# Transposing activations with VectorE and SBUF to SBUF transfers in place of TensorE transposes

## The chip, the cores and the metric

The kernel runs on one core of a Trainium2 chip. The metric is device time in microseconds (us): medians over several executions. Where two kernels are compared, the ratio is the mean time of one kernel's fast runs over that of the other's fast runs of the same rounds, with a 95% interval; it is therefore not quite the ratio of the medians that are quoted beside it.

## The reference, cut to what matters

Four layers of a graph network act on `x` of shape (32, 512, 128), all fp32: 32 graphs ("batches") of 512 nodes ("tokens") with 128 features.

```python
h = maximum(layernorm(x), 0)                      # ahead of every layer
# layer 0: attention weights A from adj, the same for every batch
x += (A * I) @ h @ W[0] + (A * (1 - I)) @ h @ W[1] + bias
# layer 1: Chebyshev hops of adj
x += relu(concat(h, adj^T h, (2 adj^2 - 1)^T h, ...) @ Theta1 + bias)
# layer 2: messages
f  = relu(h @ psi + psi_b);  m = (adj * adj)^T f
x += relu(concat(m, h) @ phi1 + phi1_b) @ phi2 + phi2_b
# layer 3: attention with a mask
s  = tanh((h @ q) @ (h @ k)^T / sqrt(128) / 8) * 8
e  = exp(s) * adj;  x += (e / e.sum(-1)) @ h @ v
```

Every product with a weight matrix sums over the features. By the code, the kernel's matmul call sums over the partitions of its operands, so `h`, which the layer norm leaves with tokens on the partitions, must first be transposed so that features are on the partitions.

## The kernel before

Sixteen pairs of batches pass through each layer, one step of a generator at a time, so that the engines work on several pairs at once. `P` and `D` are 128, `N` is 512, `NT = N // P` is 4. A pair in a layer needs 8 transposes of 128x128: TensorE makes four into one PSUM bank, and ScalarE copies the bank out to the tile `hT`, in which the 512 tokens of a batch are contiguous.

```python
def transposed(src, name, copy):
    p = bank(f"p_{name}")                          # one PSUM bank, 128 x 512 fp32
    for t in range(NT):
        nc.tensor.transpose(p[:, blk(t)], src[:, t, :], ident)
    s = work.tile([P, N], F32, tag="hT", name=name, bufs=8)
    copy(s, p)
    return s

def projected(name, *terms):                       # stationary: a block of hT
    p = bank(name)
    for t in range(NT):
        for i, (hT, w) in enumerate(terms):
            nc.tensor.matmul(p[:, blk(t)], hT[:, blk(t)], w, start=(i == 0),
                             stop=(i == len(terms) - 1))
    return tiles(p)
# ... (cut)
def layer0_first(q):                               # four pairs ahead of layer0(q)
    ln_stats(q)
    yield
    h = normed(q)
    yield
    hT = [transposed(h[:, b], f"hT0_{q}_{b}", nc.scalar.copy) for b in range(2)]
    yield
    # ... pg = projected(f"p_g_{q}_{b}", (hT[b], w0[:, 1, :])), copied to g by VectorE
def layer0(q):
    # ... hd[b] = hT[b] * adiag on GpSimd; x + bias on GpSimd
    # ... po += attT-block @ g  (p_l, 128x256), po += hd-block @ w0[:, 0, :]  (p_l, 128x128)
def layer2(q):
    h = normed(q)
    yield
    hT = [transposed(h[:, b], f"hT2_{q}_{b}", nc.scalar.copy) for b in range(2)]
    yield
    # ... pf = projected(f"p_feat_{q}_{b}", (hT[b], psi)); msgT = mixed(feat, sq)
    #     ph  = phi1[:, 1, :] @ hT[b]    moving: 512 columns of hT   (p_phi)
    #     ph += phi1[:, 0, :] @ msgT[b]
def layer3(q):
    # ... pp = qk @ hT[b]                moving: 512 columns of hT   (p_qkh)
    #     pv = projected(f"p_hv_{q}_{b}", (hT[b], vw))
    #     ps = hT[b]-block @ qkh         stationary: hT              (p_score)
```

In the profile a matmul has a stationary operand of 128x128, read by a weight load (LDWEIGHTS), and a moving operand, whose columns the MATMUL instruction reads. `hT` is used as both. Such a product of fp32 operands in the source is two instructions in the profile (`p_feat`: 128 products, x256), a transpose is one (`p_hT`: 512, x512).

Of the kernel before, what the change touches and what calls it, by code (L numbers as in the profile page):

```python
# [9 lines left out]
F32 = mybir.dt.float32  # L10
# [3 lines left out]
AX = mybir.AxisListType  # L14

P = 128
NEG = 9000000000000000.0
EPS = 1e-5
EARLY = 4
# [3 lines left out]
def kernel(  # L23
# [27 lines left out]
    nc = tc.nc  # L51
    B, N, D = x.shape
    NT = N // P
# [4 lines left out]
    const = ctx.enter_context(tc.tile_pool(name="const", bufs=1))  # L58
    xpool = ctx.enter_context(tc.tile_pool(name="xpool", bufs=NQ))
    stats = ctx.enter_context(tc.tile_pool(name="stats", bufs=NQ + 2))  # L60
    psum = ctx.enter_context(tc.tile_pool(name="psum", bufs=8, space=bass.MemoryType.PSUM))
    work = ctx.enter_context(tc.tile_pool(name="work", bufs=4))

    def bank(name):
        return psum.tile([P, 512], F32, tag="bank", name=name)

    def tiles(ap):
        return ap.rearrange("p (t f) -> p t f", f=D)

    def blk(t):  # L70
        return slice(t * P, (t + 1) * P)


    adj_s = const.tile([P, NT, N], F32, name="adj_s")
    adj_r = adj.rearrange("(t p) j -> p t j", p=P)
    for t in range(NT):
        nc.sync.dma_start(adj_s[:, t, :], adj_r[:, t, :])
# [24 lines left out]
    w0 = const.tile([P, 2, D], F32, name="w0")  # L102
# [12 lines left out]
    th = load_rows(theta, "th")  # L115
    b1 = load_bcast(bias_l1, "b1")
    psi = load_rows(psi_w, "psi")[:, 0, :]
    psib = load_bcast(psi_b, "psib")
    phi1 = load_rows(phi1_w, "phi1")
    phi1b = const.tile([P, 1], F32, name="phi1b")  # L120
    nc.sync.dma_start(phi1b, phi1_b.rearrange("(p o) -> p o", o=1))
    phi2 = load_rows(phi2_w, "phi2")[:, 0, :]
    phi2b = load_bcast(phi2_b, "phi2b")
    vw = load_rows(v_w, "vw")[:, 0, :]
# [3 lines left out]
    prep = prep_scope.enter_context(tc.tile_pool(name="prep", bufs=1))  # L128
# [10 lines left out]
    ident = const.tile([P, P], F32, name="ident")  # L139
# [42 lines left out]
                nc.scalar.activation(h[:, b], h[:, b], AF.Relu)  # L182
        return h

    def transposed(src, name, copy):
        p = bank(f"p_{name}")
        for t in range(NT):
            nc.tensor.transpose(p[:, blk(t)], src[:, t, :], ident)  # L188
        s = work.tile([P, N], F32, tag="hT", name=name, bufs=8)
        copy(s, p)  # L190
        return s

    def mixed(h, mat, tag, name, copy):

# [4 lines left out]
        copy(s, p)  # L199
        return s  # L200

    def projected(name, *terms):

        p = bank(name)
        for t in range(NT):
            for i, (hT, w) in enumerate(terms):
                nc.tensor.matmul(p[:, blk(t)], hT[:, blk(t)], w, start=(i == 0),  # L207
                                 stop=(i == len(terms) - 1))
        return tiles(p)

# [3 lines left out]
    def layer0_first(q):  # L214
        ln_stats(q)
        yield
        h = normed(q)
        yield
        hT = [transposed(h[:, b], f"hT0_{q}_{b}", nc.scalar.copy) for b in range(2)]
        yield  # L220
        g = work.tile([P, NT, 2, D], F32, tag="g", name=f"g_{q}", bufs=4)
        for b in range(2):
            pg = projected(f"p_g_{q}_{b}", (hT[b], w0[:, 1, :]))
            nc.vector.tensor_copy(g[:, :, b, :], pg)
        early[q] = hT, g

# [6 lines left out]


    adjT = const.tile([P, NT, N], F32, name="adjT")
    cheb = const.tile([P, NT, N], F32, name="cheb")

    def fillers():

# [41 lines left out]
    for t in range(NT):  # L281
        for s in range(t + 1):
            nc.tensor.matmul(pi[:, t : t + 1], upto[:, s, blk(t)], rch[:, s : s + 1],
                             start=(s == 0), stop=(s == t))
    pc = bank("p_count")
    for t in range(NT):
        nc.tensor.matmul(pc, rch[:, t : t + 1].to_broadcast([P, P]), upto[:, t, :],
                         start=(t == 0), stop=(t == NT - 1))
# [7 lines left out]
    for t in range(NT):  # L296
        s = prep.tile([P, NE], F16, tag="lt", name=f"lt_{t}", bufs=2)
# [5 lines left out]
    pg = []  # L303
    for kk in range(NK):
# [3 lines left out]
        for t in range(NT):  # L308
            nc.tensor.matmul(pb[:, kk : kk + 1], of_row[:, t, blk(kk)], befh[:, t : t + 1],
                             start=(t == 0), stop=(t == NT - 1))  # L310
# [10 lines left out]
    for kk in range(NK):  # L321
        s = prep.tile([P, N], F16, tag="scr", name=f"scr_r{kk}", bufs=2)
# [4 lines left out]
    for kk in range(NK):  # L327
        w = prep.tile([P, N], F32, tag="scan", name=f"scan_{kk}", bufs=2)
# [6 lines left out]
                                ecol[:, kk : kk + 1], OP.is_equal, OP.mult)  # L335


    att = prep.tile([P, NT, N], F32, name="att")
    diag = prep.tile([P, NT, P], F32, name="diag")
    neg_max = prep.tile([P, NT], F32, name="neg_max")  # L340
    total = prep.tile([P, NT], F32, name="total")
# [21 lines left out]
        nc.vector.tensor_sub(att[:, t, blk(t)], att[:, t, blk(t)], diag[:, t, :])  # L363

    fill(2 * EARLY + 2)
    attT = const.tile([P, NT, N], F32, tag="att_sq", name="attT")
    transpose_square(att, attT, "attT")

    adiag = const.tile([P, N], F32, name="adiag")
    p = bank("p_adiag")  # L370
    for t in range(NT):
        nc.tensor.matmul(p[:, blk(t)], ones, diag[:, t, :], start=True, stop=True)
    nc.scalar.copy(adiag, p)
    for _ in filler:
        pass

# [18 lines left out]

    def layer0(q):
        hT, g = early.pop(q)
        hd = []
        for b in range(2):
            hd.append(late.tile([P, N], F32, tag="mT", name=f"hd_{q}_{b}"))  # L400
            nc.gpsimd.tensor_mul(hd[b], hT[b], adiag)
        nc.gpsimd.tensor_add(xt[q], xt[q], b0[:, None, None, :].to_broadcast([P, 2, NT, D]))
        yield
        for t0 in range(0, NT, 2):
            po = bank(f"p_l0_{q}_{t0}").rearrange("p (t b f) -> p t b f", t=2, b=2)
            for i in range(2):
                for s in range(NT):
                    nc.tensor.matmul(po[:, i], attT[:, s, blk(t0 + i)], g[:, s], start=(s == 0), stop=False)  # L408
                for b in range(2):
                    nc.tensor.matmul(po[:, i, b], hd[b][:, blk(t0 + i)], w0[:, 0, :], start=False,  # L410
                                     stop=(b == 1))
            xv = xt[q][:, :, t0 : t0 + 2, :].rearrange("p b t f -> p t b f")
            nc.vector.tensor_add(xv, po, xv)
        ln_stats(q)

    def layer1(q):
        h = normed(q)
        yield
        hT = [transposed(h[:, b], f"hT1_{q}_{b}", nc.scalar.copy) for b in range(2)]
        x1T, x2T = [], []  # L420
        for b in range(2):
            x1T.append(mixed(h[:, b], adj_s, "mT", f"x1T_{q}_{b}", nc.vector.tensor_copy))
            x2T.append(mixed(h[:, b], cheb, "x2T", f"x2T_{q}_{b}", nc.scalar.copy))
        yield
        for b in range(2):
            po = projected(f"p_l1_{q}_{b}", (hT[b], th[:, 0, :]), (x1T[b], th12[:, 0, :]),
                           (x2T[b], th12[:, 1, :]))
            y = late.tile([P, NT, D], F32, tag="y", name=f"y1_{q}_{b}", bufs=3)
            nc.vector.tensor_add(y, po, spread(b1, NT))
            nc.vector.scalar_tensor_tensor(xt[q][:, b], y, 0.0, xt[q][:, b], OP.max, OP.add)  # L430
        ln_stats(q)

    def layer2(q):
        h = normed(q)
        yield
        hT = [transposed(h[:, b], f"hT2_{q}_{b}", nc.scalar.copy) for b in range(2)]
        yield
        feat = []
        for b in range(2):
            pf = projected(f"p_feat_{q}_{b}", (hT[b], psi))  # L440
            feat.append(late.tile([P, NT, D], F32, tag="y", name=f"feat_{q}_{b}", bufs=3))
            nc.vector.tensor_add(feat[b], pf, spread(psib, NT))
            nc.scalar.activation(feat[b], feat[b], AF.Relu)
        yield
        msgT = [mixed(feat[b], sq[0], "mT", f"msgT_{q}_{b}", nc.vector.tensor_copy) for b in range(2)]
        nc.gpsimd.tensor_add(xt[q], xt[q], phi2b[:, None, None, :].to_broadcast([P, 2, NT, D]))  # L446
        yield
        h1T = []
        for b in range(2):
            ph = bank(f"p_phi1_{q}_{b}")  # L450
            nc.tensor.matmul(ph, phi1[:, 1, :], hT[b], start=True, stop=False)  # L451
            nc.tensor.matmul(ph, phi1[:, 0, :], msgT[b], start=False, stop=True)  # L452
            h1T.append(late.tile([P, N], F32, tag="x2T", name=f"h1T_{q}_{b}"))
            nc.scalar.activation(h1T[b], ph, AF.Relu, bias=phi1b)
        yield
        for b in range(2):
            po = projected(f"p_l2_{q}_{b}", (h1T[b], phi2))
            nc.vector.tensor_add(xt[q][:, b], po, xt[q][:, b])
        ln_stats(q)

    def layer3(q):
        h = normed(q, on_act=False)
        yield
        hT = [transposed(h[:, b], f"hT3_{q}_{b}", nc.scalar.copy) for b in range(2)]
        yield
        for b in range(2):
            pp = bank(f"p_qkh_{q}_{b}")
            nc.tensor.matmul(pp, qk, hT[b], start=True, stop=True)  # L468
            qkh = late.tile([P, N], F32, tag="mT", name=f"qkh_{q}_{b}")
            nc.vector.tensor_copy(qkh, pp)  # L470

            pv = projected(f"p_hv_{q}_{b}", (hT[b], vw))
            hv = late.tile([P, NT, D + 1], F32, tag="hv", name=f"hv_{q}_{b}", bufs=3)
            nc.gpsimd.memset(hv[:, :, D : D + 1], 1.0)
            nc.vector.tensor_copy(hv[:, :, :D], pv)
            yield
            ex = late.tile([P, NT, N], F32, tag="ex", name=f"ex_{q}_{b}", bufs=3)
            for t in range(NT):
                ps = bank(f"p_score_{q}_{b}_{t}")
                nc.tensor.matmul(ps, hT[b][:, blk(t)], qkh, start=True, stop=True)  # L480
                nc.scalar.activation(ex[:, t, :], ps, AF.Tanh, scale=1.0 / (8.0 * math.sqrt(D)))  # L481
            for t in range(NT):
                nc.scalar.activation(ex[:, t, :], ex[:, t, :], AF.Exp, scale=8.0)  # L483
# [17 lines left out]
    sq = []  # L501

    def square():
        sq.append(const.tile([P, NT, N], F32, tag="att_sq", name="sq"))
        nc.gpsimd.tensor_mul(sq[0], adj_s, adj_s)
        yield

# [44 lines left out]
```

## Time and profile before

| | before |
|---|---|
| time, median of the first 3 runs | 1100.01 us (1099.19 to 1100.29) |
| TensorE busy | 1072.8 of 1096.7 us |
| VectorE, ScalarE, GpSimd busy | 489.5, 471.7, 213.3 us |

Three more of before are needed for comparison with what comes later. The first is from the chain of waits in order of time (start us, us, what), the second from the groups by form (busy us, mean ns, then idle time ahead and its cause), the third from the waits of TensorE (us in total, times, longest):

```profile
646.43 0.86 PE p_phi L451 x2
```

```profile
L207 PEld LDWEIGHTS p_feat<-psi,hT 128*128 128x128 f32 x256 | 31.0, 192 | 7.7 <-issue 7.2 <-ACT hT L190 0.5
```

```profile
PE p_g L207 <- ACT hT L190: 3.0, 3, 1.8
```

Two 512-column matmuls that stream `hT` take 0.86 us. A weight load from `hT` lasts 192 ns. In the whole run TensorE waits for transposed tiles for only 3.0 us ahead of `p_g` and 0.2 us ahead of `p_feat`.

### The profile page before, as it was taken

Reading aid. Unit: us, or ns where it says so; the run is one execution under the profiler, and the core shown is the slowest. Engines: PE = TensorE matmul, PEld = TensorE weight load, DVE = VectorE, ACT = ScalarE, POOL = GpSimd, SP = SyncE. Lnnn points to the kernel's source line nnn. Section 1 sums busy time; section 2 is a strip of 40 time slices with the busy share of each in tenths; the row PEclk is TensorE's granted clock in tenths of the full one; section 3 lists DMA queues with packets and bytes.
Section 4 is the critical chain, followed back from the end, with each engine's and each line's share of the span. In section 5 each row is a group of like instructions: output and inputs, shape, how many; then the busy total and the mean of one; then the engine's idle time right before and its main releaser. Section 6 shows DMA issues by size and latency. Waiting matters only on the chain.

```text
span 1096.7 us, 13885 instructions
## 1 busy us (share of the span) xinstructions
PE 1072.8 (98%) x5446; PEld 747.8 (68%) x5446; DVE 489.5 (45%) x1160; ACT 471.7 (43%) x997; POOL 213.3 (19%) x179
## 2 busy tenths in 40 slices
PE   5899999999999999999999999999999999999997
PEld 3579999985656656556566655666667777777776
DVE  8715555332322322323233333445475655554443
ACT  5734433502322323223264444443286656565553
POOL 3334444220000000000021111100023222222232
PEclk9999999999999999999999999999999999999999
DMA  9400000000000000000000000000000000000001
GB/s 274 115 1 1 1 1 1 1 1 1 1 1 1 1 1 1 1 1 1 1 1 1 1 0 1 1 1 1 1 11 30 30 30 30 30 30 29 30 30 39
DMA packets 37489, 19.90 MB, mean 18 GB/s; under 512 B 1840, under 2 KB 36912, under 8 KB 37424
## 3 DMA queue, kind: packets, MB, share of 16 engines
q1 hardware_dynamic: 37424, 19.01, 6.3%
q8 instruction: 43, 0.70, 0.3%
q14 instruction: 22, 0.18, 0.1%
HBM read 10.62 MB, written 8.39 MB: 17 GB/s over the span
## 4 chain that ended last, share of the span: by engine, by line
PE 94%; SPq 2%; issue 1%; ACT 1%; DMA 1%; POOL 0%; DVE 0%; POOLq 0%; DVEq 0%
PE p_l L207 10%; PE p_msgT L197 10%; PE p_x1T L197 10%; PE p_x2T L197 10%; PE p_av L492 10%; PE p_l L408 10%; PE p_score L480 10%; PE p_hT L188 5%; PE p_feat L207 3%; PE p_l L410 3%; PE p_hv L207 3%; PE p_phi L451 3%; PE p_phi L452 3%; PE p_qkh L468 2%; PE p_g L207 2%; SPq L84 2%
## 5 line engine op out<-in xcount | busy, mean ns | idle before, releaser
L176 ACT ACTIVATE h<-x,sh,rs 128x128 f32<-128x128 f32 x384 | 154.9, 486 | 3.3 <-DVE sh L166 2.3
L485 POOL TENSOR_TENSOR ex<-ex,adjT 128x512 f32<-128x512 f32 x64 | 83.5, 1306 | 230.6 <-ACT ex L483 202.0
L492 PEld LDWEIGHTS p_av<-hv,ex 128*128 128x128 f32 x1024 | 118.6, 191 | 10.3 <-issue 4.3
L446 POOL TENSOR_TENSOR x<-x,phi2b 128x1024 f32<-128x1024 f32 x16 | 38.1, 2381 | 445.0 <-ACT h L176 335.6
L492 PE MATMUL p_av<-hv,ex 128*128 128x129 f32 x1024 | 120.7, 275 | 1.5 <-POOL ex L485 1.4
L408 PE MATMUL p_l<-g,attT 128*128 128x256 f32 x512 | 121.1, 379 | 0.0
L480 PE MATMUL p_score<-qkh,hT 128*128 128x512 f32 x256 | 115.1, 592 | 0.0
L197 PE MATMUL p_x1T<-adj_s,h 128*128 128x512 f32 x256 | 115.1, 592 | 0.0
L197 PE MATMUL p_x2T<-cheb,h 128*128 128x512 f32 x256 | 115.1, 592 | 0.0
L481 ACT ACTIVATE ex<-p_score 128x512 f32<-128x512 f32 x128 | 71.9, 588 | 98.4 <-PE p_score L480 86.4
L197 PE MATMUL p_msgT<-sq,feat 128*128 128x512 f32 x256 | 112.5, 592 | 0.0
L408 PEld LDWEIGHTS p_l<-g,attT 128*128 128x128 f32 x512 | 92.4, 190 | 9.9
L190 ACT COPY hT<-p_hT 128x512 f32<-128x512 f32 x128 | 70.1, 586 | 66.5 <-PE p_hT L188 66.5
L199 ACT COPY x2T<-p_x2T 128x512 f32<-128x512 f32 x32 | 18.8, 586 | 184.4 <-PE p_x2T L197 184.4
L159 DVE BATCH_NORM_STATS2 bn<-x 128x6 f32<-128x256 f32 x256 | 94.3, 419 | 3.0 <-DMA x<-in_x_dram 0.4
L197 PEld LDWEIGHTS p_x2T<-cheb,h 128*128 128x128 f32 x256 | 48.6, 190 | 61.2 <-issue 61.2
L197 PEld LDWEIGHTS p_msgT<-sq,feat 128*128 128x128 f32 x256 | 48.6, 190 | 60.9 <-issue 56.9
L197 PEld LDWEIGHTS p_x1T<-adj_s,h 128*128 128x128 f32 x256 | 47.4, 190 | 53.6 <-issue 53.6
L480 PEld LDWEIGHTS p_score<-qkh,hT 128*128 128x128 f32 x256 | 46.2, 190 | 46.4 <-issue 42.1
L483 ACT ACTIVATE ex<-ex 128x512 f32<-128x512 f32 x128 | 76.6, 630 | 1.9
L199 DVE COPY x1T<-p_x1T 128x512 f32<-128x512 f32 x32 | 22.1, 692 | 119.2 <-PE p_x1T L197 119.2
L485 DVE TENSOR_TENSOR ex<-ex,adjT 128x512 f32<-128x512 f32 x64 | 45.8, 715 | 65.1 <-ACT ex L483 65.1
(127 smaller groups left out, 1461.8 us busy)
## 6 DMA issues: line engine op xcount, KB each, us to landing
x<-in_x_dram SPq DMA_DIRECT2D x32, 256.0 KB, 5.5
out_dram<-x SPq DMA_DIRECT2D x32, 256.0 KB, 2.3
adj_s<-in_adj_dram SPq DMA_DIRECT2D x4, 256.0 KB, 3.2
th<-in_L_gnn_Theta_dram SPq DMA_DIRECT2D x1, 320.0 KB, 6.3
w<-in_L_gnn_W_dram SPq DMA_DIRECT2D x1, 128.0 KB, 4.6
b<-in_L_gnn_bias_dram SPq DMA_DIRECT2D x2, 64.0 KB, 5.3
phi<-in_L_gnn_phi_w_dram SPq DMA_DIRECT2D x1, 128.0 KB, 3.5
qw<-in_L_gnn_q_dram SPq DMA_DIRECT2D x1, 64.0 KB, 4.2
```

The lines of the kernel that those rows point to most:

```text
L159: nc.vector.bn_stats(st[:, k].rearrange("p e s -> p (e s)"), xt[q][:, b, t : t + 2, :].rearrange("p t f -> p f t"))
L176: nc.scalar.activation(h[:, b, t, :], xt[q][:, b, t, :], AF.Relu, bias=shift[q][:, i : i + 1], scale=scale[q][:, i : i + 1])
L188: nc.tensor.transpose(p[:, blk(t)], src[:, t, :], ident)
L190: copy(s, p)
L197: nc.tensor.matmul(p, h[:, t, :], mat[:, t, :], start=(t == 0), stop=(t == NT - 1))
L207: nc.tensor.matmul(p[:, blk(t)], hT[:, blk(t)], w, start=(i == 0), stop=(i == len(terms) - 1))
L408: nc.tensor.matmul(po[:, i], attT[:, s, blk(t0 + i)], g[:, s], start=(s == 0), stop=False)
L480: nc.tensor.matmul(ps, hT[b][:, blk(t)], qkh, start=True, stop=True)
L481: nc.scalar.activation(ex[:, t, :], ps, AF.Tanh, scale=1.0 / (8.0 * math.sqrt(D)))
L483: nc.scalar.activation(ex[:, t, :], ex[:, t, :], AF.Exp, scale=8.0)
L485: eng.tensor_mul(ex[:, t, :], ex[:, t, :], adjT[:, t, :])
L492: nc.tensor.matmul(po[:, i, : D + 1], ex[:, t, blk(i0 + i)], hv[:, t, :], start=(t == 0), stop=(t == NT - 1))
```

## The change

The intent is to take the transposes from TensorE, which bounds the kernel (94% of the chain), and give them to VectorE, which is idle for more than half of the time (busy for 489.5 of 1096.7 us). In this code VectorE transposes within squares of 32x32, so each of the 16 squares of a 128x128 block is then moved to its partitions by an SBUF to SBUF transfer. To make each transfer's run of bytes long (1 KB per partition), the new tile holds the eight values of one token index (2 batches x 4 blocks) side by side. Consecutive tokens of one block are then 8 elements, or 32 bytes, apart. The core of the diff:

```diff
-    def transposed(src, name, copy):
-        p = bank(f"p_{name}")
-        for t in range(NT):
-            nc.tensor.transpose(p[:, blk(t)], src[:, t, :], ident)
-        s = work.tile([P, N], F32, tag="hT", name=name, bufs=8)
-        copy(s, p)
-        return s
+    def feature_major(name):
+        return work.tile([P, P, 2, NT], F32, tag="hT", name=name, bufs=4)
+    def in_order(hT):
+        return hT.rearrange("p n t -> p t n")
+    def transposed_by_pe(h, name):
+        # ... as before, with nc.scalar.copy(in_order(hT[:, :, b, :]), tiles(p))
+    def transposed(h, name):
+        hb = late.tile([P, NQR, QR, 2, NT], F32, tag="hb", name=f"hb_{name}", bufs=2)
+        for b in range(2):
+            nc.vector.transpose(hb[:, :, :, b, :].rearrange("p j r t -> p t j r"),
+                                h[:, b].rearrange("p t (j c) -> p t j c", c=QR))
+        hT = feature_major(name)
+        for i in range(NQR):
+            for j in range(NQR):
+                nc.sync.dma_start(hT[j * QR : (j + 1) * QR, i * QR : (i + 1) * QR],
+                                  hb[i * QR : (i + 1) * QR, j])
+        return hT
+    def at(hT, b):
+        return lambda t: hT[:, :, b, t]
 # projected: stationary hT(t) in place of hT[:, blk(t)]
 # layer0_first:
-        hT = [transposed(h[:, b], f"hT0_{q}_{b}", nc.scalar.copy) for b in range(2)]
+        hT = (transposed_by_pe if q < EARLY else transposed)(h, f"hT0_{q}")
 # layers 1, 2, 3: hT = transposed(h, ...) and one more yield
 # layer 2 (layer 3 likewise for p_qkh):
-            nc.tensor.matmul(ph, phi1[:, 1, :], hT[b], start=True, stop=False)
+            nc.tensor.matmul(ph, phi1[:, 1, :], in_order(hT[:, :, b, :]), start=True, stop=False)
```

The diagonal products `hd` take the same layout, and the four large square tiles (`adj_s`, `cheb`, `att`/`sq`, `ex`) now share a set of four buffers.

More of the change, by code (lines that the diff above doesn't have):

```diff
@@ L16 @@
 P = 128
+QR = 32
+NQR = P // QR
 NEG = 9000000000000000.0
@@ L62 @@
     work = ctx.enter_context(tc.tile_pool(name="work", bufs=4))
+    bounce = ctx.enter_context(tc.tile_pool(name="bounce", bufs=4, space=bass.MemoryType.DRAM))
     def bank(name):
@@ L71, in blk, with square_tile @@
         return slice(t * P, (t + 1) * P)
-    adj_s = const.tile([P, NT, N], F32, name="adj_s")
+    def square_tile(name):
+        return const.tile([P, NT, N], F32, tag="square", name=name, bufs=4)
+    adj_s = square_tile("adj_s")
     adj_r = adj.rearrange("(t p) j -> p t j", p=P)
@@ L183, in normed @@
         return h
-    def transposed(src, name, copy):
-        p = bank(f"p_{name}")
-        for t in range(NT):
-            nc.tensor.transpose(p[:, blk(t)], src[:, t, :], ident)
-        s = work.tile([P, N], F32, tag="hT", name=name, bufs=8)
-        copy(s, p)
-        return s
+    def feature_major(name):
[5 more added lines that the diff above has]
+        for b in range(2):
+            p = bank(f"p_{name}_{b}")
+            for t in range(NT):
+                nc.tensor.transpose(p[:, blk(t)], h[:, b, t, :], ident)
+            nc.scalar.copy(in_order(hT[:, :, b, :]), tiles(p))
+        return hT
+    def transposed(h, name):
+        hb = late.tile([P, NQR, QR, 2, NT], F32, tag="hb", name=f"hb_{name}", bufs=2)
+        for b in range(2):
+            nc.vector.transpose(hb[:, :, :, b, :].rearrange("p j r t -> p t j r"),
+                                h[:, b].rearrange("p t (j c) -> p t j c", c=QR))
+        hT = feature_major(name)
+        for i in range(NQR):
+            for j in range(NQR):
+                nc.sync.dma_start(hT[j * QR : (j + 1) * QR, i * QR : (i + 1) * QR],
+                                  hb[i * QR : (i + 1) * QR, j])
+        return hT
     def mixed(h, mat, tag, name, copy):
@@ L200, in mixed, with columns @@
         return s
+    def at(hT, b):
+        return lambda t: hT[:, :, b, t]
+    def columns(xT):
+        return lambda t: xT[:, blk(t)]
     def projected(name, *terms):
@@ L206, in projected @@
             for i, (hT, w) in enumerate(terms):
-                nc.tensor.matmul(p[:, blk(t)], hT[:, blk(t)], w, start=(i == 0),
+                nc.tensor.matmul(p[:, blk(t)], hT(t), w, start=(i == 0),
                                  stop=(i == len(terms) - 1))
@@ L222, in layer0_first @@
         for b in range(2):
-            pg = projected(f"p_g_{q}_{b}", (hT[b], w0[:, 1, :]))
+            pg = projected(f"p_g_{q}_{b}", (at(hT, b), w0[:, 1, :]))
             nc.vector.tensor_copy(g[:, :, b, :], pg)
@@ L235 @@
     adjT = const.tile([P, NT, N], F32, name="adjT")
-    cheb = const.tile([P, NT, N], F32, name="cheb")
+    cheb = square_tile("cheb")
     def fillers():
@@ L335 @@
                                 ecol[:, kk : kk + 1], OP.is_equal, OP.mult)
-    att = prep.tile([P, NT, N], F32, name="att")
+    att = square_tile("att")
     diag = prep.tile([P, NT, P], F32, name="diag")
@@ L365 @@
     fill(2 * EARLY + 2)
-    attT = const.tile([P, NT, N], F32, tag="att_sq", name="attT")
+    attT = square_tile("attT")
     transpose_square(att, attT, "attT")
-    adiag = const.tile([P, N], F32, name="adiag")
+    adiag = const.tile([P, P, NT], F32, name="adiag")
     p = bank("p_adiag")
@@ L372 @@
         nc.tensor.matmul(p[:, blk(t)], ones, diag[:, t, :], start=True, stop=True)
-    nc.scalar.copy(adiag, p)
+    nc.scalar.copy(in_order(adiag), tiles(p))
     for _ in filler:
@@ L397, in layer0 @@
         hT, g = early.pop(q)
-        hd = []
-        for b in range(2):
-            hd.append(late.tile([P, N], F32, tag="mT", name=f"hd_{q}_{b}"))
-            nc.gpsimd.tensor_mul(hd[b], hT[b], adiag)
+        hd = late.tile([P, P, 2, NT], F32, tag="hd", name=f"hd_{q}", bufs=2)
+        nc.gpsimd.tensor_mul(hd, hT, adiag[:, :, None, :].to_broadcast([P, P, 2, NT]))
         nc.gpsimd.tensor_add(xt[q], xt[q], b0[:, None, None, :].to_broadcast([P, 2, NT, D]))
@@ L409, in layer0 @@
                 for b in range(2):
-                    nc.tensor.matmul(po[:, i, b], hd[b][:, blk(t0 + i)], w0[:, 0, :], start=False,
+                    nc.tensor.matmul(po[:, i, b], hd[:, :, b, t0 + i], w0[:, 0, :], start=False,
                                      stop=(b == 1))
@@ L418, in layer1 @@
         yield
-        hT = [transposed(h[:, b], f"hT1_{q}_{b}", nc.scalar.copy) for b in range(2)]
+        hT = transposed(h, f"hT1_{q}")
+        yield
         x1T, x2T = [], []
@@ L425, in layer1 @@
         for b in range(2):
-            po = projected(f"p_l1_{q}_{b}", (hT[b], th[:, 0, :]), (x1T[b], th12[:, 0, :]),
-                           (x2T[b], th12[:, 1, :]))
+            po = projected(f"p_l1_{q}_{b}", (at(hT, b), th[:, 0, :]), (columns(x1T[b]), th12[:, 0, :]),
+                           (columns(x2T[b]), th12[:, 1, :]))
             y = late.tile([P, NT, D], F32, tag="y", name=f"y1_{q}_{b}", bufs=3)
@@ L435, in layer2 @@
         yield
-        hT = [transposed(h[:, b], f"hT2_{q}_{b}", nc.scalar.copy) for b in range(2)]
+        hT = transposed(h, f"hT2_{q}")
+        yield
         yield
@@ L439, in layer2 @@
         for b in range(2):
-            pf = projected(f"p_feat_{q}_{b}", (hT[b], psi))
+            pf = projected(f"p_feat_{q}_{b}", (at(hT, b), psi))
             feat.append(late.tile([P, NT, D], F32, tag="y", name=f"feat_{q}_{b}", bufs=3))
@@ L456, in layer2 @@
         for b in range(2):
-            po = projected(f"p_l2_{q}_{b}", (h1T[b], phi2))
+            po = projected(f"p_l2_{q}_{b}", (columns(h1T[b]), phi2))
             nc.vector.tensor_add(xt[q][:, b], po, xt[q][:, b])
@@ L463, in layer3 @@
         yield
-        hT = [transposed(h[:, b], f"hT3_{q}_{b}", nc.scalar.copy) for b in range(2)]
+        hT = transposed(h, f"hT3_{q}")
+        yield
         yield
@@ L467, in layer3 @@
             pp = bank(f"p_qkh_{q}_{b}")
-            nc.tensor.matmul(pp, qk, hT[b], start=True, stop=True)
+            nc.tensor.matmul(pp, qk, in_order(hT[:, :, b, :]), start=True, stop=True)
             qkh = late.tile([P, N], F32, tag="mT", name=f"qkh_{q}_{b}")
             nc.vector.tensor_copy(qkh, pp)
-            pv = projected(f"p_hv_{q}_{b}", (hT[b], vw))
+            pv = projected(f"p_hv_{q}_{b}", (at(hT, b), vw))
             hv = late.tile([P, NT, D + 1], F32, tag="hv", name=f"hv_{q}_{b}", bufs=3)
@@ L476, in layer3 @@
             yield
-            ex = late.tile([P, NT, N], F32, tag="ex", name=f"ex_{q}_{b}", bufs=3)
+            ex = square_tile(f"ex_{q}_{b}")
             for t in range(NT):
                 ps = bank(f"p_score_{q}_{b}_{t}")
-                nc.tensor.matmul(ps, hT[b][:, blk(t)], qkh, start=True, stop=True)
+                nc.tensor.matmul(ps, hT[:, :, b, t], qkh, start=True, stop=True)
                 nc.scalar.activation(ex[:, t, :], ps, AF.Tanh, scale=1.0 / (8.0 * math.sqrt(D)))
@@ L503, in square @@
     def square():
-        sq.append(const.tile([P, NT, N], F32, tag="att_sq", name="sq"))
+        sq.append(square_tile("sq"))
         nc.gpsimd.tensor_mul(sq[0], adj_s, adj_s)
```

## The prediction

> **What bounds the kernel now.** I read the page first: busy shares, the slices, the chain that ended last. Then I asked for the chain in order of time inside one layer, the groups by form, and the transfer queue's timeline.
>
> ```profile
> PE 1072.8 (98%) x5446; PEld 747.8 (68%) x5446; DVE 489.5 (45%) x1160; ACT 471.7 (43%) x997; POOL 213.3 (19%) x179
> PE   5899999999999999999999999999999999999997
> PEclk9999999999999999999999999999999999999999
> PE 94%; SPq 2%; issue 1%; ACT 1%; DMA 1%; POOL 0%; DVE 0%; POOLq 0%; DVEq 0%
> ```
>
> TensorE is busy for 1072.8 of 1096.7 us, in every slice from the third to the last but one, at full clock, and the chain is 94% TensorE. No other engine reaches half the span. So a microsecond of TensorE work removed is a microsecond of time, unless something new makes TensorE wait; work moved to VectorE is free while its results come in time.
>
> How much are the transposes? In the groups by form:
>
> ```profile
> L188 PE MATMUL p_hT<-ident,h 128*128 128x128 f32 x512 | 67.0, 274 | 0.0
> L190 ACT COPY hT<-p_hT 128x512 f32<-128x512 f32 x128 | 70.1, 586 | 66.5 <-PE p_hT L188 66.5
> L159 DVE BATCH_NORM_STATS2 bn<-x 128x6 f32<-128x256 f32 x256 | 94.3, 419 | 3.0 <-DMA x<-in_x_dram 0.4
> ```
>
> 274 ns is the latency of one pipelined transpose, and 67.0 us counts its overlap with its neighbours. What a transpose holds TensorE for is read from the chain in order of time (here a stretch of layer 2; columns: start, us, what):
>
> ```profile
> 649.87 6.87 PE p_msgT L197 x16
> 656.73 1.78 PE p_feat L207 x16
> 658.52 0.87 PE p_hT L188 x8
> ```
>
> Eight transposes advance the chain by 0.87 us, 109 ns each; 16 matmuls of 128 columns by 1.78 us, 111 ns each (each product in the source is two of these instructions); 512 columns cost 6.87/16 = 429 ns. All are back to back.
>
> [...]
> - [...] No VectorE transpose is in this trace, so its duration is an estimate below.
> - [...] Here each is 32 partitions x 1 KB = 32 KB. [...] a 64 KB load takes 0.43 us to issue, a 0.5 KB one 0.47 us.
> - [...] The new layout puts consecutive tokens 32 bytes apart, so this is my main risk. The trace speaks partly against it: the batch-norm statistics above read neighbours 512 bytes apart, and 256 elements take 419 ns. VectorE's scalar_tensor_tensor rows, which read without such a stride, take 346 ns for 128 columns and 700 ns for 512, so 0.92 ns a column and about 464 ns for 256. No penalty on VectorE. TensorE reads nothing with such a stride before.
>
> **The change part by part.**
> *Removed.* There are 16 pairs in 4 layers, so 64 groups of 8 transposes; the first 4 groups of layer 0 stay on TensorE. 60 groups go: 60 x 0.87 = **52.2 us off TensorE, all on the path**. Also 120 ScalarE copies x 586 ns = 70 us, off the path.
>
> *Added on VectorE.* 120 transposes of 128x512. Other 128x512 instructions on VectorE take 0.69 to 0.72 us; estimate 0.7 us each, 84 us in all. VectorE goes from 489 to about 575 us of some 1050. Even at 1.3 us each it stays near 650, so it does not become the bound.
>
> *Added transfers.* 60 x 16 = 960, 31 MB, all issued by SP. Issue rates from the queue's timeline (start, us, what):
>
> ```profile
> 10.08 0.43 SPq L89 DMA_DIRECT2D qw<-in_L_gnn_q_dram  x1
> 10.56 0.43 SPq L89 DMA_DIRECT2D kw<-in_L_gnn_k_dram  x1
> ```
>
> A start every 0.48 us. Sixteen take about 7.6 us, plus about 2.3 us until the last has landed (the output stores' median): **a group arrives about 10 us after its VectorE transposes**. SP issues for 960 x 0.48 = 460 us, below half the span. Is 10 us hidden?
>
> - Layers 1 to 3: the instruction order of the built program puts consumers far behind. Layer 1 computes the 16+16 matmuls of 429 ns (13.7 us) of its own pair before the first use, and a round is 19.9 - 0.87 = 19 us. Layers 2 and 3 have an empty step more. In layer 3 a buffer of the transposed pair comes free at the last score matmul of the pair four earlier; until first use stand three av groups (3.57 us each), two more score groups (3.44) and three qkh+hv groups (1.75), so about 23 us against 10. Hidden.
> - Layer 0 is tightest. A round is 11.35 us now and 10.5 after. The transposes of pair k+4 stand around the first residual add of pair k, done about 1.4 us after that half's matmuls. Transfers land at 1.4 + 10 = 11.4 us. TensorE still has the other half of pair k (4.4), p_g of the pair ahead (1.8) and all of pair k+1 (8.7) before it wants the data: 14.9 us. Slack about 3.5 us.
>
> *Moved.* The square for layer 2 [...] now has its own slot, and the scheduler puts it just ahead of the first diagonal product hd. It starts when the attention transposes end (65.0 us), so hd (2.4 us) is ready at about 72.5, where TensorE now wants it at 69.1 and waits 0.7 us: **about 2.7 us of new wait, once**. [...] I count 1.5 us for all first uses together.
>
> *Changed in place.* 1280 weight loads (p_g, layer-1 term, p_feat, p_hv, hd: 256 each), 256 score weight loads, and 128 512-column moving operands (p_phi, p_qkh) now read with a 32-byte step. I count 0, because fp32 matmuls stream 512 columns in 429 ns, 0.84 ns a column, close to the 0.92 ns at which VectorE reads such steps free.
>
> Sum: 1100.0 - 52.2 + 2.7 + 1.5 = **1052 us**.
>
> **The rivals.**
> 1. *Strided reads slow TensorE.* If a weight load took twice its 107 ns or so of back-to-back spacing, the 1280 matmuls of 128 columns would be bound by it: 1280 x 0.107 = 137 us, and moving operands at half rate 128 x 0.43 = 55 us: up to about 1240 us. With 20% on both, 27 + 11 = 38 us, and the gain is nearly gone (1090). [...] Against it: the VectorE row. I give 17% to a large penalty, 15% to a small one.
> 2. *Transfers come late.* If SP needs 0.9 us per transfer, as for the 256 KB x loads (24 in 21.1 us), a group takes 16.7 us; layer 0 is late by some 3 us per round, 12 rounds, 36 us: 1088. Against it: those loads move eight times the bytes and small ones issue in 0.43. The other layers still hide 17 us.
> 3. *VectorE becomes the wait.* Its order is fixed, and a transpose waits for the transfers of two groups before; then evictions behind it come late and PSUM fills. Against it: eight banks, with the transposes' use of them gone. Perhaps 5 to 10 us.
>
> **Range and chances.** Without a stride penalty the parts allow 1045 to 1065; a small penalty gives 1065 to 1090; a large one leaves the range. So 1043 to 1090 holds about 8 in 10. Faster by over 2% means below 1078: 0.77. Within 2%: 0.10. Slower: 0.13.
>
> **What would show each step.** In the profile after: TensorE busy near 1020 us with 4966 matmuls, and no gap at the first use of a transposed tile except in the first diagonal product. p_feat x16 still at 1.78 us and p_phi at 0.86 per two: then strides are free; a p_feat of 2.1 or 3.5 us is rival 1. SP starts 0.4 to 0.5 us apart and no wait of p_g on a transfer: else rival 2. A VectorE transpose near 0.7 us. ScalarE down by 70 us without effect. A strided-read penalty, which nothing in this trace can exclude, would make the prediction wrong.

## The result, and the profile after

The changed kernel takes **1260.45 us** (median of 4 runs, 1258.40 to 1261.06) against 1100.15 us (4 runs) for the kernel before in the same rounds. The ratio is 1.1447, with a 95% interval of 1.142 to 1.1475. The prediction of 1052 us was wrong by 208 us, and in the wrong direction.

The same lines of the page as in the prediction (busy time and share of each engine; TensorE's busy tenths in 40 slices; its clock; shares of the chain):

```profile
PE 1234.6 (98%) x4966; PEld 885.4 (70%) x4966; DVE 607.2 (48%) x1280; ACT 414.7 (33%) x877; POOL 208.9 (17%) x163
PE   5999999999999999999999999999999999999998
PEclk9999999999999999999999999999999999999999
PE 94%; DVE 2%; issue 1%; SPq 1%; DMA 1%; POOL 0%; ACT 0%; POOLq 0%; DVEq 0%
```

TensorE has the 480 instructions fewer that were promised (4966 for 5446), and yet it is busy for 162 us longer. The clock is the same. The chain is TensorE's as before, so nothing else took the bound over. The time must lie in the duration of its own instructions. The chain in order of time, in layer 2:

```profile
751.50 6.87 PE p_msgT L225 x16
758.37 3.69 PE p_feat L241 x16
762.06 1.79 PE p_l L241 x16
763.84 1.83 PE p_phi L485 x2
765.67 0.86 PE p_phi L486 x2
```

This stretch compares the instructions side by side. `p_msgT`, `p_l` (from `h1T`) and the second `p_phi` (L486, from `msgT`) read contiguous operands and take exactly what they took before. `p_feat`, whose stationary operand is the new tile, takes 3.69 us for 16 where it took 1.78: 231 ns each for 111. The first `p_phi`, whose moving operand is the new tile, takes 1.83 us for two where it took 0.86. The groups by form add the weight loads and VectorE's new work:

```profile
L212 DVE STREAM_TRANSPOSE hb_hT<-h 128x512 f32<-128x512 f32 x120 | 131.3, 1102 | 137.8 <-ACT h L182 86.5 <-DMA hT<-hb_hT 35.9 <-PE p_qk L421 14.9
L241 PEld LDWEIGHTS p_feat<-psi,hT 128*128 128x128 f32 x256 | 63.3, 332 | 5.3 <-issue 3.3 <-DMA hT<-hb_hT 0.2
L241 PEld LDWEIGHTS p_l<-phi,h1T 128*128 128x128 f32 x256 | 30.1, 193 | 0.0
```

A weight load from the new tile lasts 332 ns, one from the contiguous `h1T` 193. VectorE's transpose takes 1.10 us where 0.7 was estimated, off the path. Its 35.9 us of waits for transfers are, by the code, waits for one of the two buffers of `hb` to come free; among the waits of TensorE's matmuls, which the trace lists down to 0.3 us, none is for such a transfer, and its weight loads list one, of 0.2 us.

Counted by rows, the 1280 matmuls with a strided stationary operand cost 119 ns more each, 152 us; the 128 with a strided moving operand 486 ns more each, 62 us; `p_score` about 4 us (3.56 us for 8, 3.44 before). That is 218 us. The transposes are gone (52 us), so 1100 + 218 - 52 = 1266 us, close to the 1260 measured. Still, this is arithmetic on rows, and two things beside the stride are new while these instructions run: the transfers and VectorE's transposes use SBUF too. The experiments separate them.

### The profile page after: what moved, and what is told of

Read it like the earlier page. It is cut to its first block, busy times and chain, and to the rows that moved or that the text cites. A ratio compares the mean times of both kernels' runs of the same rounds, so it can differ in the third digit from the quotient of the medians.

```text
span 1259.3 us, 14324 instructions
## 1 busy us (share of the span) xinstructions
PE 1234.6 (98%) x4966; PEld 885.4 (70%) x4966; DVE 607.2 (48%) x1280; ACT 414.7 (33%) x877; POOL 208.9 (17%) x163
## 4 chain that ended last, share of the span: by engine, by line
PE 94%; DVE 2%; issue 1%; SPq 1%; DMA 1%; POOL 0%; ACT 0%; POOLq 0%; DVEq 0%
PE p_l L241 11%; PE p_score L515 9%; PE p_l L440 9%; PE p_msgT L225 9%; PE p_av L527 9%; PE p_x1T L225 8%; PE p_x2T L225 8%; PE p_g L241 5%; PE p_feat L241 5%; PE p_phi L485 5%; PE p_qkh L503 5%; PE p_l L442 4%; PE p_hv L241 4%; PE p_phi L486 2%; PE p_cheb L290 1%
## 5 line engine op out<-in xcount | busy, mean ns | idle before, releaser
L212 DVE STREAM_TRANSPOSE hb_hT<-h 128x512 f32<-128x512 f32 x120 | 131.3, 1102 | 137.8 <-ACT h L182 86.5
L515 PE MATMUL p_score<-qkh,hT 128*128 128x512 f32 x256 | 119.0, 608 | 0.0
L241 PEld LDWEIGHTS p_hv<-vw,hT 128*128 128x128 f32 x256 | 65.9, 330 | 42.2 <-issue 30.1
L515 PEld LDWEIGHTS p_score<-qkh,hT 128*128 128x128 f32 x256 | 78.2, 317 | 22.5 <-issue 0.2
L168 ACT ACTIVATE sd<-bn,eps 128x8 f32<-128x8 f32 x64 | 18.0, 299 | 227.8 <-DVE bn L165 227.7
L165 DVE BATCH_NORM_STATS2 bn<-x 128x6 f32<-128x256 f32 x256 | 91.2, 409 | 1.3
L520 DVE TENSOR_TENSOR ex<-ex,adjT 128x512 f32<-128x512 f32 x64 | 52.9, 827 | 68.5 <-ACT ex L518 68.3
L241 PE MATMUL p_l<-th,hT 128*128 128x128 f32 x256 | 79.4, 392 | 0.0
```

What stands on the lines that cost most here:

```text
L165: nc.vector.bn_stats(st[:, k].rearrange("p e s -> p (e s)"), xt[q][:, b, t : t + 2, :].rearrange("p t f -> p f t"))
L212: nc.vector.transpose(hb[:, :, :, b, :].rearrange("p j r t -> p t j r"), h[:, b].rearrange("p t (j c) -> p t j c", c=QR))
L241: nc.tensor.matmul(p[:, blk(t)], hT(t), w, start=(i == 0), stop=(i == len(terms) - 1))
L515: nc.tensor.matmul(ps, hT[:, :, b, t], qkh, start=True, stop=True)
L520: eng.tensor_mul(ex[:, t, :], ex[:, t, :], adjT[:, t, :])
```

## The experiments

**Theories.** A: TensorE's strided operand reads alone cost the time. B: the transfers or VectorE's transposes slow TensorE, or make it wait. C: the transfers are late once TensorE is fast, so part of the gain would be lost even without the stride. Twelve kernels were run. Runs 1 to 4 were timed on one chip and runs 5 to 12 on another; the median of the kernel before lay between 1099.86 and 1101.29 us in their rounds, so a difference of 1 or 2 us between runs of different rounds is not taken for an effect. In runs 1 to 3 and 5 every transpose is back on TensorE, and only the tile's layout varies:

```diff
+S = 4          # or 2, or 1: elements between consecutive tokens (the changed kernel: 8)
     def feature_major(name):
-        return work.tile([P, P, 2, NT], F32, tag="hT", name=name, bufs=4)
+        return work.tile([P, 2, NT // S, P, S], F32, tag="hT", name=name, bufs=4)
-        hT = transposed(h, f"hT1_{q}")          # and in the other layers
+        hT = transposed_by_pe(h, f"hT1_{q}")
```

**Run 1: the stride alone (32 bytes), no transfers.** Only the second part of the diff.

> The changed kernel's layout of the transposed tile (tokens 32 bytes apart) with all transposes back on TensorE: no VectorE transpose and no SBUF to SBUF transfer is left. Theory A, the strided operand reads of TensorE cost the time: the 52 us of transposes come back on top, so about 1260 + 52 = 1312 us; p_feat x16 stays at 3.7 us and p_phi from hT at 1.83 us per two in the chain. Theory B, the transfers or VectorE's transposes (their SBUF traffic, or waits for them) slow TensorE: with them gone it falls to about 1100 us, p_feat x16 back to 1.78.

Measured: 1314.43 us, ratio to before 1.1955 (1.1938 to 1.1973). The chain in order of time, in layer 2, as for the next two runs:

```profile
665.41 3.67 PE p_feat L241 x16
669.08 0.87 PE p_hT L203 x8
669.95 1.83 PE p_phi L485 x2
```

Without any transfer or VectorE transpose, the strided instructions are as slow as in the changed kernel, and the transposes come on top. Theory B falls: it wanted 1100 us.

**Run 2: 16 bytes between tokens.** `S = 4`.

> As the first, with tokens 16 bytes apart instead of 32. Theory A1, [...] all of the penalty stays, about 1312 us, p_feat x16 at 3.7. Theory A2, the penalty grows with the distance: half of the 212 us of stride cost goes, about 1206 us, p_feat x16 near 2.7. Theory A3, it sets in only above 16 bytes: about 1100 us. Theory B (transfers): 1100 us.

Measured: 1304.62 us, ratio 1.1865 (1.1847 to 1.1883).

The chain:

```profile
658.45 3.61 PE p_feat L245 x16
...
662.93 1.80 PE p_phi L490 x2
```

Half the distance wins back only 10 us: near the number of A1 (1312), not those of A2 (1206) or A3 (1100).

**Run 3: 8 bytes between tokens.** `S = 2`.

> As the first, with tokens 8 bytes apart[...]. Theory A1 [...]: about 1100 us, p_feat x16 at 1.78 us. Theory A2 (grows with distance): about 1150 us, p_feat x16 near 2.2. Theory A4 (any stride but 1 costs): about 1312 us, p_feat x16 at 3.7.

Measured: 1110.61 us, ratio 1.0105 (1.009 to 1.012).

The chain:

```profile
769.29 1.88 PE p_feat L246 x16
...
773.83 0.90 PE p_phi L491 x2
```

At 8 bytes the penalty is nearly gone: 118 ns a matmul instead of 111 and 450 ns for 512 columns instead of 429. So the step from 8 to 16 bytes costs 194 us, the one from 16 to 32 another 10. ScalarE's copies out of PSUM, which write the same layouts, show the same edge in the groups by form (the first line is of run 2, the second of run 3):

```profile
L208 ACT COPY hT<-p_hT 128x512 f32<-128x512 f32 x128 | 131.6, 1111 | 74.0 <-PE p_hT L207 74.0
```

```profile
L208 ACT COPY hT<-p_hT 128x512 f32<-128x512 f32 x128 | 74.3, 626 | 32.2 <-PE p_hT L207 32.2
```

**Run 4: the change itself with contiguous tokens.** `S = 1`, VectorE transposes and transfers kept; a transfer moves 8 runs of 128 bytes per partition in place of one of 1 KB.

```diff
-            nc.vector.transpose(hb[:, :, :, b, :].rearrange("p j r t -> p t j r"),
+            nc.vector.transpose(hb[:, :, b, :, :, 0].rearrange("p j t r -> p t j r"),
-                nc.sync.dma_start(hT[j * QR : (j + 1) * QR, i * QR : (i + 1) * QR],
+                nc.sync.dma_start(hT[j * QR : (j + 1) * QR, :, :, i * QR : (i + 1) * QR],
```

> The changed kernel with the tokens of a transposed tile contiguous (as the kernel before has them), VectorE transposes and transfers kept; a transfer then moves runs of 128 bytes in place of 1 KB. Theory A (the stride is the whole of what the prediction missed): p_feat x16 back at 1.78 us and the time about 1052 us, if the transfers stay hidden. Theory C (the transfers are late once TensorE is fast): a group is issued in 16 x 0.65 = 10.4 us against a layer 0 round of 10.5 us, [...] so p_g waits on a transfer in layer 0, some us per round of 12 rounds: 1065 to 1100 us. Theory B: 1260 us as after. The VectorE transpose falls from 1.10 us to about 0.7 if it was its strided write that cost.

Measured: 1058.85 us, ratio 0.9627 (0.9611 to 0.9643). This is 202 us faster than the changed kernel and 3.7% faster than before. It lies 7 us above 1052, as theory C has it. From the groups by form, then three stretches of the chain in order of time in layer 0:

```profile
L216 DVE STREAM_TRANSPOSE hb_hT<-h 128x512 f32<-128x512 f32 x120 | 82.2, 699 | 105.4 <-ACT h L183 83.5 <-PE p_qk L425 16.5 <-issue 3.6
```

```profile
93.27 0.61 SPq L221
93.88 0.04 issue
93.92 0.61 SPq L221
...
100.20 2.48 DMA hT<-hb_hT
102.68 0.04 DVEq L216
102.72 0.12 DVE sh L173
102.83 0.15 issue
102.98 2.67 PE p_g L245 x16
...
168.28 2.02 PE p_g L245 x16
...
179.47 2.02 PE p_g L245 x16
```

VectorE's transpose falls from 1.10 to 0.70 us: its writes paid for the 32-byte step too. The chain now runs through SP's issues: one transfer every 0.65 us, 16 of them 10.4 us at that rate, plus 2.5 us for the last to land; then, after 0.3 us on VectorE, `p_g`, which takes 2.67 us and later 2.02 where it took 1.79. The delay isn't the same in every round: several rounds after this first one are 10.5 us long as planned, those late in the layer up to 11.4 (179.47 - 168.28 = 11.2).

To see where the gain is lost, the chain in order of time is cut at the end of the last `p_attT` and at the first `p_x1T`, `p_msgT` and `p_qkh` in it (us; each column is one profiled execution). Layer 2's first `p_feat` falls ahead of its cut:

| stage | before | after | run 1 | run 4 | run 5 | run 7 | run 8 | run 9 |
|---|---|---|---|---|---|---|---|---|
| up to the last `p_attT` | 64.6 | 73.0 | 74.3 | 66.1 | 66.6 | 66.2 | 68.1 | 66.4 |
| layer 0 | 175.8 | 215.9 | 227.3 | 174.9 | 176.4 | 177.2 | 171.6 | 165.0 |
| layer 1 | 322.6 | 340.4 | 357.0 | 308.7 | 323.6 | 308.7 | 308.7 | 308.7 |
| layer 2 | 226.4 | 270.8 | 283.9 | 213.5 | 226.5 | 213.5 | 213.5 | 213.5 |
| layer 3 | 303.9 | 355.8 | 369.3 | 291.6 | 303.0 | 291.6 | 291.6 | 291.6 |

Layers 1 to 3 of run 4 win 39 us of the 48 x 0.87 = 41.8 due. Layer 0 wins 0.9 of the 12 x 0.87 = 10.4 due.

**Run 5: the control.** All transposes on TensorE, `S = 1`.

> The control of the first three: all transposes on TensorE, tokens contiguous, but the new tiles, the moved square and the rest of the change kept. Theory A (stride alone): within 0.5% of before, 1098 to 1105 us, with p_feat x16 at 1.78 us; what it stands above 1100 is what the rest of the change costs (the prediction had 2.7 us for the square ahead of the first diagonal product). If something else in the change cost time too, it stands well above 1105.

Measured: 1101.33 us, ratio 1.0009 (0.9982 to 1.0036).

The same stretch of the chain:

```profile
763.57 1.78 PE p_feat L245 x16
...
768.01 0.86 PE p_phi L490 x2
```

So nothing else that this run keeps of the change costs time that can be seen. The stride alone, run 1 less run 5, is 213 us.

**Run 6: transfers kept, 8 bytes between tokens.** `S = 2`, with four VectorE transposes of 128x256 per pair in place of two of 128x512.

> As the fourth run (VectorE transposes and transfers kept), with tokens 8 bytes apart: a transfer moves runs of 256 bytes, and VectorE makes twice as many transposes of half the size. Theory A: the 8-byte step costs what the third run showed, 1280 x 6 ns + 128 x 20 ns = 10 us, on top of the 1059 us of the fourth, so about 1069. If short runs of bytes are what cost the fourth run its 7 us over 1052, this one wins some of that back: about 1065. A VectorE transpose of 128x256 near 0.35 us if 8 bytes are free for its writes, near 0.55 if not.

Measured: 1063.61 us, ratio 0.9654 (0.9635 to 0.9674). It lies 3 us above run 4 by the ratios and 5 by the medians, which come from different rounds, but not 10. The strided reads cost what run 3 showed (1.88 us for 16 `p_feat` and 0.90 us for two `p_phi` in the chain, as there), but layer 0 takes 172.2 us, 2.7 less than in run 4. Whether the longer runs of 256 bytes or the slightly longer rounds do that isn't settled. A VectorE transpose of half the size took 0.43 us in the chain, more than half of 699 ns; the runs don't separate the size from the step. VectorE's scalar_tensor_tensor rows of before take 346 ns for 128 columns and 700 for 512, so there too a smaller instruction takes more than its share.

**Run 7: layer 0 on TensorE, layers 1 to 3 as in run 4.**

```diff
-        hT = (transposed_by_pe if q < EARLY else transposed)(h, f"hT0_{q}")
+        hT = transposed_by_pe(h, f"hT0_{q}")
```

> The fourth run's kernel with layer 0 wholly on TensorE (12 groups more of 0.87 us, 10.4 us). Theory C1 (the 7 us that the fourth run stands above 1052 are waits on SP's issue in layer 0): these waits go, TensorE is idle for about as long as before in layer 0, and the time is 1059 - 7 + 10.4 = 1062 us. Theory C2 (the 7 us lie elsewhere, or are spread over all layers): 1059 + 10.4 = 1069 us.

Measured: 1062.04 us, ratio 0.9641 (0.9625 to 0.9657). The number is C1's. The 12 groups put back cost only 2 to 3 us in the whole (by the ratios, by the medians), because the waits go: layer 0 takes 177.2 us, 1.4 more than before, and its `p_g` groups are at 1.79 us each again. What run 4 lost, it lost in layer 0.

**Run 8: three of layer 0's twelve groups on TensorE.**

```diff
-        hT = (transposed_by_pe if q < EARLY else transposed)(h, f"hT0_{q}")
+        hT = (transposed_by_pe if q < EARLY or q % 4 == 0 else transposed)(h, f"hT0_{q}")
```

> The fourth run's kernel with every fourth group of layer 0 (three of its twelve) back on TensorE: 2.6 us more of TensorE work, and SP has 39 us for three groups of 10.4 us. Theory C1 (SP's issue bounds layer 0): 1059 - 7 + 2.6 = about 1055 us. Theory C2: 1059 + 2.6 = 1062 us.

Measured: 1059.12 us, ratio 0.9612 (0.9594 to 0.963). This misses C1's 1055 and lies between the theories. Layer 0 does shrink, to 171.6 us, but 168.0 were due (165.4 + 2.6), and the preparation ended 2 us later in this profile. A group that still goes by transfers costs SP its full 10.4 us at once, and the chain still passes through 14 issues in a row, now for the first pair after the one put back. They start behind a bias addition on GpSimd there, so this run alone doesn't settle C1. Spreading the load over rounds didn't remove the late arrival.

**Run 9: a second queue issues a quarter of layer 0's transfers.** Run 4 with:

```diff
-    def transposed(h, name):
+    def transposed(h, name, other=None):
-                nc.sync.dma_start(...)
+                (other if other and i == 3 else nc.sync).dma_start(...)
-        hT = (transposed_by_pe if q < EARLY else transposed)(h, f"hT0_{q}")
+        hT = transposed_by_pe(h, f"hT0_{q}") if q < EARLY else transposed(h, f"hT0_{q}", nc.scalar)
```

> The fourth run's kernel, but in layer 0 a quarter of the transfers (4 of 16 in a group) is issued by ScalarE's queue in place of SP's. The stages of the chain put the 7 to 8 us that the fourth run lost into layer 0 (174.9 us, where 166.8 was due). Theory C1 (SP's issue, 10.4 us per group against a round of 10.5): SP needs 7.8 us per group, the waits go, and layer 0 takes about 167 to 169 us: the whole about 1052 us. Theory C3 (the transfers' own time or the first-use waits, whoever issues): stays at about 1059 us. ScalarE is busy for 39 of 95 us in this stretch, so 4 issues of 0.6 us in a round should not show.

Measured: **1051.14 us** (5 runs, 1050.97 to 1053.36), ratio to before 0.9548 (0.953 to 0.9566). The chain in order of time in layer 0:

```profile
172.09 1.79 PE p_g L245 x16
...
182.57 1.79 PE p_g L245 x16
```

The round is 10.48 us, `p_g` is back at 1.79 us, and layer 0 takes 165.0 us, where 175.8 - 10.4 = 165.4 were due. C1 is shown: issuing all transfers through SP's queue was the bound of layer 0. The runs don't separate SP's own issuing from its queue. Relieving it was worth 8 us.

**Run 10: half of them on ScalarE's queue** (`i >= 2`).

> As the last, with half of layer 0's transfers on ScalarE's queue: SP 5.2 us per group, ScalarE 5.2 us more per round of 10.5, about 9.5 in all. Theory C1: layer 0 at about 167 us, 1051 us, unless ScalarE's own activations come late behind the issues (then 1055 or more). Theory C3: 1059 us.

Measured: 1051.32 us, ratio 0.9546 (0.9527 to 0.9565), layer 0 165.0 us. As run 9; ScalarE had the room.

**Run 11: that half on GpSimd's queue** (`nc.gpsimd`).

> As the last, with that half on GpSimd's queue, which in layer 0 also makes the diagonal products and the bias additions (about 4.9 us per round). Theory C1: about 1051 us, if an issue costs GpSimd no more than the 0.6 us that it costs SP; at 1 us or more each (8 per round), the products hd come late and it is 1060 or worse. Theory C3: 1059 us.

Measured: 1052.15 us, ratio 0.9548 (0.9533 to 0.9564), layer 0 165.0 us. GpSimd is busy for 55.8 us more with 96 issues of 589 ns, and TensorE's waits for it are those of run 9 (1.6 us for `hd`, 2.0 us for `ex`). Runs 9, 10 and 11 can't be told apart.

**Run 12: only the moving operands strided, 512 bytes apart.** Run 5 with the columns of `p_phi` and `p_qkh` read in another order, one from each of the four blocks in turn. Its output is wrong, which doesn't matter for the time.

```diff
-            nc.tensor.matmul(ph, phi1[:, 1, :], in_order(hT[:, b]), start=True, stop=False)
+            nc.tensor.matmul(ph, phi1[:, 1, :], hT[:, b].rearrange("p a n s -> p n a s"), start=True, stop=False)
```

> The control of the fifth run with one thing changed: the 128 moving operands of 512 columns (p_phi, p_qkh) are read from the contiguous tile in another order, so that consecutive reads lie 512 bytes apart; the stationary operands stay contiguous. The order of the columns is wrong for what follows, so the result is wrong on purpose. If the moving reads pay by themselves [...]: p_phi x2 at 1.8 us, p_feat x16 at 1.78, and 1101 + 128 x 0.486 = about 1163 us; the stationary reads then make the other 151 of the 213 us between the first and the fifth run. If the distance counts, 512 bytes cost more than 32: p_phi x2 well above 1.83. If only stationary reads pay: about 1101 us.

Measured: 1158.48 us, ratio 1.0527 (1.0508 to 1.0545).

The same stretch of the chain:

```profile
703.65 1.78 PE p_feat L245 x16
...
708.10 1.74 PE p_phi L490 x2
```

The moving reads pay by themselves, 57 us (run 12 less run 5), and the stationary ones stay at 1.78. At run 1's step the same 128 instructions cost 62 us by rows, so 151 to 156 us of its 213 are the stationary operands'. A step of 512 bytes costs no more than one of 32 (1.74 us for two against 1.83), so the distance isn't what counts. The comparison with the reference accepted this wrong kernel: its tolerance doesn't see the permuted terms, so it would not catch such an error in these two operands.

## Why the prediction was wrong, point by point

- **What bounds the kernel** was right. TensorE bounds both kernels, with 94% of the chain, and in run 9 the 52.2 us of TensorE work removed took 49.9 us off the four layers.
- **Removed: 52.2 us.** Right. Run 9's four layers are 10.8, 13.9, 12.9 and 12.3 us shorter than before, 49.9 in all, where 10.4 and three times 13.9 were due. The 2.3 us between lie in layers 2 and 3 and were not traced.
- **Changed in place: "I count 0".** This is the step that failed. It measured 209 us (the changed kernel less run 9) or 213 us (run 1 less run 5), and the difference of 4 us was not pursued. The argument for 0 was a row of VectorE, whose statistics read neighbours 512 bytes apart at no visible cost (419 ns for 256 elements). Run 12 gives TensorE that step and it takes twice the time. The row was not a like case, for two reasons that the runs don't separate. It is another engine. And by the code (`p t f -> p f t` over two rows) its reads alternate between two rows 512 bytes apart, where run 12 goes round four blocks and the new tile moves on by 32 bytes at each token. "No penalty on VectorE" was the estimate from other instructions' times; no run has the contiguous read to compare. VectorE isn't free of the cost either: its transposes, writing with the 32-byte step, took 1.10 us for 0.70.
- **The main risk** was named: the prediction put it on the 32-byte step, and then gave more weight to the row of another engine. Runs 1, 2, 3 and 12 price it. With 8 bytes between tokens a matmul with a strided stationary operand takes 118 ns, with 16 bytes 226, with 32 bytes 231, where a contiguous one takes 111; a strided moving operand of 512 columns takes 450, 900 and 915 ns, and 870 at 512 bytes, where a contiguous one takes 429. Why the edge lies between 8 and 16 bytes the runs don't show.
- **Rival 1** was therefore the truth, in mechanism and nearly in size: it put 137 us on the stationary and 55 on the moving operands; the runs show 151 to 156 and 57 to 62. The error was its weight, 17% for a large penalty. The trace of before holds no such read of TensorE, so it could not price the step; run 1, the altered layout alone, does.
- **VectorE's transposes: 0.7 us.** Mis-sized at 1.10 us, because their writes have the 32-byte step; 0.70 us when contiguous. Off the path in both cases, as predicted.
- **The transfers: 10 us for a group.** Mis-sized: an issue comes every 0.65 us, not 0.48, so a group needs about 12.9 us (10.4 + 2.5). The slack of 3.5 us in layer 0 was too hopeful; the likely reason is that the next group's issue also queues behind it: with 10.4 us of issue in a round of 10.5 SP had none to spare. In the changed kernel this was hidden by the slower matmuls: its layer 0 takes 215.9 / 16 = 13.5 us a pair. It showed at once when TensorE was fast (run 4), and cost 8 us. Rival 2 named it, with a larger size (36 us). For layers 1 to 3, "hidden" was right.
- **Rival 3** came about in part and off the path: in the changed kernel VectorE's transposes waited 35.9 us for transfers, and the one place where the chain leads through such a wait cost TensorE 0.8 us (`p_l` behind `x2T`). In run 4 such waits are at most 1.8 us in all (the idle time ahead of its transposes, 105.4 us, less the 83.5, 16.5 and 3.6 us that its row puts down to other causes).
- **The square ahead of the first product: 2.7 us.** Run 5 shows 0.6 us more in layer 0, and no difference in the whole that its interval can tell. In the trace of before the square itself lasts 3.60 us.
- **The 1052 us** were right for a kernel that nobody had written yet. Run 9, with a contiguous tile and a second queue, takes 1051. That they agree to 1 us is partly luck, since the 2.7 us added for the square weren't found and the late transfers were left out; the 1.5 us for first uses were the author's estimate and were not measured by themselves. And the question was about the kernel with the stride.

## What to carry to other kernels

When a change alters the layout of what the bounding engine reads, price the new step of every operand on that engine first; here a step of 8 bytes nearly kept TensorE's speed (118 ns a matmul for 111) and one of 16 bytes halved it (226). A layout chosen to make transfers long did not pay: with runs of 128 bytes in place of 1 KB the transfers were hidden in layers 1 to 3, and in layer 0 with a second queue, and the kernel took 200 us less. After a bound has been relaxed, look at whatever has a period close to the new round, as SP's issue had (10.4 us in a round of 10.5), and split it over a second queue.

## What these runs measured

- A step of 8 bytes was nearly free for TensorE's stationary operands, one of 16 was not: 16 matmuls take 1.78 us contiguous (run 5), 1.88 at 8 bytes (run 3) and 3.61 at 16 (run 2).
- A TensorE matmul with a strided stationary operand goes from 111 to 231 ns at 32 bytes (its weight load from 192 to 332 ns), a moving operand of 512 columns from 429 to 915 ns, a ScalarE copy of 128x512 that writes with 16 or 32 bytes from 589 to 1111 ns, a VectorE transpose of 128x512 that writes with 32 bytes from 699 to 1102 ns. VectorE's statistics, whose reads alternate between two rows 512 bytes apart, took 419 ns for 256 elements.
- An fp32 transpose on VectorE took 699 ns for 128x512 (run 4) and 0.43 us for 128x256, the latter written with an 8-byte step (run 6).
- In run 4 SP issued one 32 KB SBUF to SBUF transfer every 0.65 us; in run 11 each issue took 589 ns of GpSimd's time.
